# Spreading the background work of a deformable convolution over its units, and finding the largest offset in one pass

## The chip, the cores and the metric

The kernel runs on one core of a Trainium2 chip. The metric is the device time of one execution in microseconds (us). Before the change it is 6298.04 us, the median of three runs (6293.81 to 6311.7). The profile that is shown comes from one profiled execution with a span of 6287.0 us.

## The reference

The input x has 4 images of 128 x 128 pixels and 128 channels, in f32. Four layers follow each other. Each normalises its input by groups of 4 channels, computes something, and adds the result to its input:

```
x = x + relu(deform_conv(gn(x), w_off, b_off, w_def))   # layer 0
x = x + scan_conv1d(gn(x), W)                           # layer 1
x = x + z_self + z_m + z_k                              # layer 2
x = x + triangle(gn(x), ...)                            # layer 3
```

Only layer 0 is touched. It computes, for each pixel, 72 offsets (4 groups of channels x 9 taps x two directions) by a 1x1 convolution of the normalised image:

```
offset = einsum('bchw,oc->bohw', gn(x), w_off) + b_off
val    = bilinear samples of gn(x) at (y + ky - 1 + dy, x + kx - 1 + dx)
out    = relu(einsum('bgckhw,ogck->bohw', val, w_def))
```

A bilinear sample whose offset is at most 1 in size needs only neighbouring pixels. The kernel relies on that. It keeps the largest absolute offset that occurred, and where it is over 1 it computes the layer again by a general path (`deform_general`).

## The kernel before

`deform_layer` works through 172 **blocks**: 4 images of 43 blocks, each of `RY` = 3 rows of the output. A block has `NU` = 4 **units** (L720). In each unit TensorE samples a quarter of the block's columns for all nine taps (`sample_unit`, L525), and ScalarE and VectorE copy the samples out of PSUM into `ring` (L551, L549). Then come the weights of two or three taps of the next block (`next_taps`, which calls `tents`): TensorE makes two factors in `t_ps` (L500, L508), ScalarE copies one of them to SBUF (`tent`, L514), and VectorE multiplies them into `m` (L516). `t_ps` has two buffers, and the next block's `sample_unit` needs all nine taps of `m`. Last comes a quarter of the convolution of the block before (L608). At the end of a block, VectorE adds that convolution's result to the image (`finish`, L578, which writes `x1c`) and so frees its one PSUM buffer, `conv_ps`.

Beside the blocks runs work for later blocks and later layers. Python generators hand it out in small pieces, and the calls in the unit loop (L724 to L732) set how many pieces a unit gets:

- **Preparing rows** (`prepared`, called through `step`). It makes the table of normalised pixels and the offsets of 8 rows, in two groups of 4 rows. A group has seven pieces: four transposes (L403), the normalisation to `rows` (L405), the offset matmul (L416), the scaling on VectorE and GpSimd (L419, L422), and three pieces that split the f32 offsets into three bf16 parts (ScalarE L432, VectorE L434 and L440, GpSimd L438). The first split piece also takes the maximum of the group's offsets, the second the minimum (L434). The two groups and one empty call make 15 steps for 8 rows. `ready[b]` is the number of rows of image `b` that are prepared.
- **Counting the next image** (`count_of`, advanced by `next(beside["count"], None)`). It loads an image in 16 halves of 16 rows into one buffer, `xhalf`, and takes 16 statistics instructions (`bn_stats`, L344) of each half. A half has six pieces: four that only leave time for the transfer, and two of 8 `bn_stats`. Preparing an image can begin once it is counted and `scales_of` has run, which goes through `step` as well.
- **Counting the layer's own output** (`count`, L592). Each 16 rows of output put 32 `bn_stats` into a list, and `count(n)` takes up to n of them. At the first block of the next image the list is emptied.

The order of the instructions on each engine is the order in which the program emits them (`manual_schedule`, L700). After the last block, L761 to L774 reduce `ranges` to a flag that says whether an offset was over 1.

Of the kernel before, what the change touches and what calls it, by code (L numbers as in the profile page):

```python
# [10 lines left out]
F32 = mybir.dt.float32  # L11
# [3 lines left out]
ALU = mybir.AluOpType  # L15
AX = mybir.AxisListType
# [3 lines left out]
P = 128  # L20
B = 4
S = 128
NG = 4
NK = 9
NL = NK * NG
# [3 lines left out]
PADW = S + 2  # L29
# [10 lines left out]
RY, RX = 3, 4  # L40
# [148 lines left out]
def deform_layer(tc, c, small, x, w_off, b_off, w_def, x1, tabs, offs):  # L189
# [11 lines left out]
    nc = tc.nc  # L201
    RC = 16
    RP = 8
    RO = 4
    NROWS = 1 + NG * NPART
    NB = RY * PADW
    with ExitStack() as ctx:
        wp = ctx.enter_context(tc.tile_pool(name="l0w", bufs=1))
# [14 lines left out]
        nc.tensor.matmul(wsum_ps, lhsT=woff, rhs=c.ones[:, 0:1], start=True, stop=True)  # L223
        wsum = wp.tile([2 * NL, 1], F32, name="wsum")
        nc.vector.tensor_copy(wsum, wsum_ps)
        ranges = wp.tile([2 * NL, 2, B * S // RO], F32, name="ranges")

# [4 lines left out]
        with tc.tile_pool(name="l0prep", bufs=1) as prep:  # L234
# [14 lines left out]
            for d in range(2):  # L249
                for place in range(RX):  # L250
                    for after, factors in ((-1, (-1, 1, 0)), (0, (1, -2, 1)), (1, (0, 1, 0))):
                        at = place + 1 + after
# [14 lines left out]
            for q in range(4):  # L267
                p0 = 32 * q
                nc.scalar.dma_start(spread[p0 : p0 + 1, q % 2], picks[0:1, q // 2, 2])
                for n in range(NPART):  # L270
                    p1 = p0 + 1 + n
                    nc.scalar.dma_start(
                        spread[p1 : p0 + NROWS : NPART, q % 2], picks[:, q // 2, n // NSPLIT]
                    )
# [44 lines left out]
        for t in pixels:  # L319
            nc.vector.memset(t, 0.0)  # L320

        ring = wp.tile([P, 3 * RY, NK, PADW], F32, name="ring")

        def ring_rows(n, r0, r1):
            at = (n * RY + r0) % (3 * RY)
            return ring[:, at : at + r1 - r0]

        parts = wp.tile([2 * NL, NPART, RP, OW], BF16, name="parts")
# [53 lines left out]
        def load_group(n):  # L382

            if n not in loaded and n < B * S // RO:
                b, y = n * RO // S, n * RO % S
                loaded[n] = three.tile([P, RO, S], F32, name="xin")
                nc.sync.dma_start(loaded[n], x[b, :, y : y + RO, :])

        def prepared(b, y0):

            s, t, st, koff = scales[b]
            table = tabs[b].rearrange("x (r s) c -> x r s c", s=SX)
            for h in range(0, RP, RO):
                n = (b * S + y0 + h) // RO
                load_group(n)
                load_group(n + 1)
                load_group(n + 2)
                xc = loaded.pop(n)
                if h == 0:
                    rows = one.tile([P, 2 * RO, P], F32, name="rows")  # L400
                pt = ps_g.tile([P, RO, P], F32, name="img_ps", tag="gn_ps")
                for i in range(RO):
                    nc.tensor.transpose(pt[:, i], xc[:, i, :], c.ident)  # L403
                yield
                nc.scalar.activation(rows[:, h : h + RO], pt, AF.Identity, bias=t, scale=s)  # L405
                if h + RO == RP:
                    for q in range(RX):
                        src = rows[q:S:RX]
                        for x0, at in ((0, q + 2), (1, q - 2)):
                            if at >= 0:  # L410
                                nc.sync.dma_start(
                                    table[x0 : x0 + NXB - 1, 2 + y0 : 2 + y0 + RP, at, :], src
                                )
                yield
                po = ps_g.tile([2 * NL, RO, S], F32, name="off_ps", tag="gn_ps")
                nc.tensor.matmul(po, lhsT=woff, rhs=xc, start=True, stop=True)  # L416
                yield
                off = one.tile([2 * NL, RO, S], F32, name="off")
                nc.vector.tensor_tensor(  # L419
                    off, po, st[:, 0].unsqueeze(1).to_broadcast([2 * NL, RO, S]), ALU.mult  # L420
                )
                nc.gpsimd.tensor_tensor(  # L422
                    off, off, koff.unsqueeze(1).to_broadcast([2 * NL, RO, S]), ALU.add
                )
                yield
                flat = off.rearrange("p r c -> p (r c)")

                rest = one.tile([2 * NL, RO, S], F32, name="rest")
                left = off
                for i in range(NSPLIT):  # L430
                    part = parts[:, i, h : h + RO, 2 : S + 2]
                    nc.scalar.copy(part, left)  # L432
                    if i < 2:
                        nc.vector.tensor_reduce(  # L434
                            ranges[:, i, n : n + 1], flat, AX.X, (ALU.max, ALU.min)[i]
                        )
                    if i + 1 < NSPLIT:
                        nc.gpsimd.tensor_tensor(rest, left, part, ALU.subtract)  # L438
                        left = rest
                    nc.vector.scalar_tensor_tensor(  # L440
                        parts[:, NSPLIT + i, h : h + RO, 2 : S + 2], off, 0.0, part,
                        ALU.is_gt, ALU.mult,
                    )
                    yield
            at = (y0 + 2) * OW
            nc.sync.dma_start(
                offs[b].rearrange("(l n) c -> l n c", n=NPART)[:, :, at : at + RP * OW],
                parts.rearrange("l n r c -> l n (r c)"),
            )
            ready[b] = y0 + RP  # L450

        def load_parts(t, b, j, rows, taps):

            for d in range(2):
                for kx in range(3):
# [3 lines left out]
                    nc.sync.dma_start(  # L459
                        t[p0 : p0 + NROWS - 1, k0 : k0 + len(taps)].rearrange(  # L460
                            "p k r c -> p k (r c)"
# [128 lines left out]
        def count(n):  # L590
            for _ in range(min(n, len(to_count))):
                nc.vector.bn_stats(*to_count.pop(0))  # L592
# [23 lines left out]
        def terms_of(n, j):  # L616

            if j == 0:
                return 0, 1, [(ky, 0, ring_rows(n, ky, ky + 1)) for ky in (2, 1, 0)]
            terms = []  # L620
            for ky in (2, 1, 0):
                at = 0
                for r0, r1 in ((ky - 2, 0), (0, ky + 1)) if n % 3 == 0 else ((ky - 2, ky + 1),):
                    if r0 < r1:
                        terms.append((ky, at, ring_rows(n, r0, r1)))
                        at += r1 - r0
            return RY * j - 2, RY * j + 1, terms
# [5 lines left out]
        ready = [0] * B  # L633
        beside = {"now": None, "norms": [], "rows": 0, "count": iter(())}
# [77 lines left out]
        for n, (b, j) in enumerate(blocks):  # L712
            load_row(n + 2)
            if n + 1 < len(blocks):
                pixel_tiles[n + 1] = load_pixels(*blocks[n + 1])
            pix = pixel_tiles.pop(n)
            m = ms.pop(("m", n)).rearrange("p r k c -> p (r k) c")
            end = j + 1 == NYB
            v = ring_rows(n, 0, RY).rearrange("p r k c -> p (r k) c")
            for i in range(NU):  # L720
                sample_unit(m, pix, v, i)
                next_taps(2)
                next(convs, None)
                for _ in range(4 if ready[b] < min(S, RY * j + 26) else 2):  # L724
                    step()
                next_taps((i == 0) + (end and i > 0))
                count(12)
                if not (j == 0 and i == 0):
                    for _ in range(2):
                        next(beside["count"], None)  # L730
                elif b + 1 < B:
                    beside["count"] = counting(b + 1)  # L732
            for _ in convs:
                pass
            if j == 0:
                if b:
                    count(len(to_count))
                    beside["norms"].append(x1_norm(b - 1, stats))
                stats = one.tile([P, NGN, S // RC, 6], F32, name="stats1")
            if not end:  # L740
                convs = convolved(b, *terms_of(n, j), stats, NU)
            else:
                ve = one.tile([P, 1, 3, PADW], F32, name="ve")
                sample_row(ms.pop(("me", n))[:, 0], pix, ve[:, 0])
                convs = chain(
                    convolved(b, *terms_of(n, j), stats, NU // 2),
                    convolved(
                        b, S - 1, S,
                        [(2, 0, ve), (1, 0, ring_rows(n, 2, 3)), (0, 0, ring_rows(n, 1, 2))],
                        stats, NU // 2,  # L750
                    ),
                )
# [5 lines left out]
            pass  # L758


        ends = wp.tile([2 * NL, 2], F32, name="ends")  # L761
        nc.vector.tensor_reduce(ends[:, 0:1], ranges[:, 0], AX.X, ALU.max)
        nc.vector.tensor_reduce(ends[:, 1:2], ranges[:, 1], AX.X, ALU.min)
        most = wp.tile([2 * NL, 1], F32, name="most")
        nc.vector.scalar_tensor_tensor(most, ends[:, 1:2], -1.0, ends[:, 0:1], ALU.mult, ALU.max)
        most_ps = ps_g.tile([1, 2 * NL], F32, name="most_ps", tag="gn_ps")
        nc.tensor.matmul(
            most_ps, lhsT=most, rhs=c.ident[0 : 2 * NL, 0 : 2 * NL], start=True, stop=True
# [711 lines left out]
```

## Time and profile before

The page's shares are over the whole span; layer 0 is about half of it. The table has the stretches that matter. A block ends where VectorE makes its one copy of line 553, so the times of those 172 copies in the trace give the length of every block.

| what | value |
|---|---|
| PE, DVE, ACT, POOL busy, whole span | 85%, 55%, 39%, 16% |
| ends of the first and the last block | 211.9 us, 3273.3 us |
| TensorE clock granted, whole span | 0.934 |
| one tensor_reduce of line 434, 72 x 512 f32 | 672 ns, 256 of them |
| one bn_stats of line 344 or 592 | 209 ns, 768 and 1024 of them |
| transposes, off matmuls of a group of 4 rows | line 403 and line 416, 128 groups |

[...] twelve bn_stats in a row take 1.60 us in the timeline, which is 0.13 us each.

### The profile page before, as it was taken

Reading aid. Unit: us, or ns where it says so; the run is one execution under the profiler, and the core shown is the slowest. Engines: PE = TensorE matmul, PEld = TensorE weight load, DVE = VectorE, ACT = ScalarE, POOL = GpSimd, SP = SyncE. Lnnn points to the kernel's source line nnn. Section 1 sums busy time; section 2 is a strip of 40 time slices with the busy share of each in tenths; the row PEclk is TensorE's granted clock in tenths of the full one; section 3 lists DMA queues with packets and bytes.
Section 4 is the critical chain, followed back from the end, with each engine's and each line's share of the span. In section 5 each row is a group of like instructions: output and inputs, shape, how many; then the busy total and the mean of one; then the engine's idle time right before and its main releaser. Section 6 shows DMA issues by size and latency. Waiting matters only on the chain. (4 is left out here: it accounts for less than half of the span.)

```text
span 6287.0 us, 157182 instructions
## 1 busy us (share of the span) xinstructions
PE 5363.7 (85%) x67400; PEld 4503.6 (72%) x67400; DVE 3485.6 (55%) x7296; ACT 2422.6 (39%) x4709; POOL 990.9 (16%) x714
## 2 busy tenths in 40 slices
PE   0689899889889898999998999998787887877876
PEld 0577778777778777788887888887474674664765
DVE  6576666666666666655544444445547446446442
ACT  0344454445444454444431111111433534434433
POOL 0211221112220122100000000000205114114122
PEclk9899998999999999999999999999998988989987
DMA  3575655665556565544432112211515416316314
GB/s 115 125 158 127 138 133 126 146 131 129 134 132 129 114 138 130 121 92 83 90 77 85 62 60 67 68 65 47 172 44 194 139 49 207 121 56 209 111 60 134
DMA packets 1264569, 710.30 MB, mean 113 GB/s; under 512 B 844621, under 2 KB 1111150, under 8 KB 1254646
## 3 DMA queue, kind: packets, MB, share of 16 engines
q1 hardware_dynamic: 1234322, 658.55, 41.3%
q10 hardware_dynamic: 29540, 41.60, 1.9%
q8 instruction: 532, 8.72, 0.6%
q14 instruction: 175, 1.43, 0.1%
HBM read 417.28 MB, written 282.55 MB: 111 GB/s over the span
## 5 line engine op out<-in xcount | busy, mean ns | idle before, releaser
L608 PE MATMUL conv_ps<-ring,wdef 128*128 128x192 f32 (+2 forms) x7632 | 1342.3, 326 | 75.7 <-DVE x1c L578 75.7
L608 PEld LDWEIGHTS conv_ps<-ring,wdef 128*128 128x128 f32 x7632 | 1168.2, 199 | 189.5 <-issue 103.5
L516 DVE TENSOR_TENSOR m<-t_ps,tent 128x390 f32<-128x390 f32 x1548 | 814.3, 559 | 803.9 <-ACT tent L514 774.6
L1075 PE MATMUL conv_ps<-carry,wconv 128*128 128x256 f32 x4572 | 1011.3, 378 | 0.3 <-issue 0.3
L1075 PEld LDWEIGHTS conv_ps<-carry,wconv 128*128 128x128 f32 x4572 | 852.1, 189 | 121.9 <-issue 0.6
L500 PE MATMUL t_ps<-parts_of,spread 57*64 57x99 bf16 (+1 forms) x12384 | 801.3, 277 | 105.5 <-DVE m L516 80.9
L525 PE MATMUL v_ps<-m,pixels 60*64 60x108 f32 (+1 forms) x22704 | 770.8, 267 | 114.8 <-DVE m L516 104.0
L514 ACT COPY tent<-t_ps 128x390 f32<-128x390 f32 x1560 | 709.7, 492 | 358.7 <-PE t_ps L500 356.3
L551 ACT COPY ring<-v_ps 128x432 f32<-128x432 f32 x1032 | 503.8, 523 | 855.1 <-PE v_ps L525 849.0
L525 PEld LDWEIGHTS v_ps<-m,pixels 60*64 60x64 f32 x22704 | 635.4, 138 | 271.0 <-DVE m L516 134.1
L500 PEld LDWEIGHTS <-spread 57*64 57x64 bf16 x12480 | 643.2, 127 | 192.1 <-issue 168.4
L1057 ACT ACTIVATE rowT<-x1T_ps,t_x,s_x 128x128 f32<-128x128 f32 x512 | 192.2, 457 | 864.6 <-PE x1T_ps L1053 417.0
L1320 PEld LDWEIGHTS pair_ps<-wcat,X 128*128 128x128 f32 x4096 | 474.2, 192 | 37.2 <-DVE T L1326 14.6
L1320 PE MATMUL pair_ps<-wcat,X 128*128 128x128 f32 x4096 | 494.8, 279 | 5.5 <-POOL X L1307 3.6
L508 PE MATMUL t_ps<-parts_of,spread 57*64 57x130 bf16 x9288 | 497.1, 227 | 0.0
L1326 DVE TENSOR_TENSOR T<-pair_ps,sig 128x512 f32<-128x512 f32 x256 | 266.6, 1044 | 398.0 <-ACT sig L1325 397.8
L422 POOL TENSOR_TENSOR off<-off,koff 72x512 f32<-72x512 f32 x128 | 163.0, 1273 | 1948.1 <-DVE off L419 1948.1
L1228 POOL TENSOR_TENSOR zc<-z 128x1024 f32<-128x1024 f32 x64 | 130.0, 2032 | 1824.2 <-DVE z L1221 1728.8
L1086 DVE SCALAR_TENSOR_TENSOR carry<-conv_ps,rowT 128x256 f32<-128x256 f32 x254 | 107.3, 423 | 540.4 <-PE conv_ps L1075 540.4
L508 PEld LDWEIGHTS <-spread 57*64 57x64 bf16 x9312 | 393.0, 109 | 0.0
L1390 PE MATMUL one_ps<-outw,y 128*128 128x128 f32 x1024 | 249.8, 333 | 150.5 <-POOL y L1384 150.0
L440 DVE SCALAR_TENSOR_TENSOR parts<-off,parts 72x512 bf16<-72x512 f32 x384 | 341.4, 891 | 28.4 <-ACT parts L432 21.2
(179 smaller groups left out, 6204.7 us busy)
## 6 DMA issues: line engine op xcount, KB each, us to landing
pixels<-tab SPq DMA_DIRECT2D x688, 123.8 KB
parts_of<-off SPq DMA_DIRECT2D x1032, 55.7 KB
off<-parts SPq DMA_DIRECT2D x64, 891.0 KB
tab<-rows SPq DMA_DIRECT2D x384, 128.0 KB
xin<-in_x_dram SPq DMA_DIRECT2D x128, 256.0 KB
x<-x1c SPq DMA_DIRECT2D x32, 1024.0 KB
x1rows<-x SPq DMA_DIRECT2D x128, 256.0 KB
x2T<-x2c ACTq DMA_DIRECT2D x128, 256.0 KB
```

Source lines behind the costliest of these rows:

```text
L440: nc.vector.scalar_tensor_tensor(parts[:, NSPLIT + i, h : h + RO, 2 : S + 2], off, 0.0, part, ALU.is_gt, ALU.mult,)
L500: nc.tensor.matmul(tp[h : h + HALF, 0, 0:n].rearrange("p (r c) -> p r c", c=PADW)[:, :, i:PADW:RX], lhsT=spread[0:k, kx // 2, i, h : h + H ...
L508: nc.tensor.matmul(tp[h : h + HALF, 1, i * PADW : (i + 1) * PADW], lhsT=spread[HALF : HALF + k, kx // 2, first + i, h : h + HALF], rhs=src ...
L514: nc.scalar.copy(tent[:, 0:n], tp[:, 0, 0:n])
L516: nc.vector.tensor_tensor(m, *pair, ALU.mult)
L525: nc.tensor.matmul(to[p1 : p1 + HALF], lhsT=pix[p0 : p0 + LANES, xb, :], rhs=m[p0 : p0 + LANES, :, RX * xb : RX * xb + w], start=True, sto ...
L551: nc.scalar.copy(to, bodies[side])
L608: nc.tensor.matmul(pc[:, at : at + rows, x0:x1], lhsT=wdef[:, side, k, :], rhs=v[:, :, k if v.shape[2] == NK else kx, x0 + kx : x1 + kx], ...
L1075: nc.tensor.matmul(pc, lhsT=wt[:, k, :], rhs=old[h][:, :, k : k + S], start=(k == 0), stop=(k == TAPS - 1),)
L1320: nc.tensor.matmul(pj[:, j], lhsT=X[:, j0 + j, :], rhs=wcat[:, q * 4 * DQ : (q + 1) * 4 * DQ], start=True, stop=True,)
L1326: nc.vector.tensor_tensor(T[:, q : NQ + 1 : NQ - q, :, j0 : j0 + JB], pj[:, :, 0 : 2 * DQ].rearrange("p j (n d) -> p n d j", n=2), sig.rea ...
L1390: nc.tensor.matmul(po[:, j], lhsT=y[:, j], rhs=outw, start=False, stop=True)
```

## The change

The change does four things in layer 0, all in `deform_layer`.

- The work for the output's statistics is taken two instructions per unit and not up to twelve.
- The count of the next image gets one piece per unit and not two.
- When fewer rows are ready than the lead asks for, a unit takes three steps of preparing and not four. The lead is 18 rows ahead of the block and not 26. Otherwise a unit takes two steps, as before.
- The largest offset is found by one maximum over absolute values. The minimum of each group goes, and with it one reduce and one combination after the last block. `ranges` shrinks to half.

The number of row sets in the ring gets a name, `NRING` = 3, with the same value.

```
-        ranges = wp.tile([2 * NL, 2, B * S // RO], F32, name="ranges")
+        ranges = wp.tile([2 * NL, B * S // RO], F32, name="ranges")
...
-                    if i < 2:
+                    if i == 0:
                         nc.vector.tensor_reduce(
-                            ranges[:, i, n : n + 1], flat, AX.X, (ALU.max, ALU.min)[i]
+                            ranges[:, n : n + 1], flat, AX.X, ALU.max, apply_absolute_value=True
                         )
...
                 next_taps(2)
                 next(convs, None)
-                for _ in range(4 if ready[b] < min(S, RY * j + 26) else 2):
+                for _ in range(3 if ready[b] < min(S, RY * j + 18) else 2):
                     step()
                 next_taps((i == 0) + (end and i > 0))
-                count(12)
+                count(2)
                 if not (j == 0 and i == 0):
-                    for _ in range(2):
-                        next(beside["count"], None)
+                    next(beside["count"], None)
                 elif b + 1 < B:
                     beside["count"] = counting(b + 1)
...
-        ends = wp.tile([2 * NL, 2], F32, name="ends")
-        nc.vector.tensor_reduce(ends[:, 0:1], ranges[:, 0], AX.X, ALU.max)
-        nc.vector.tensor_reduce(ends[:, 1:2], ranges[:, 1], AX.X, ALU.min)
         most = wp.tile([2 * NL, 1], F32, name="most")
-        nc.vector.scalar_tensor_tensor(most, ends[:, 1:2], -1.0, ends[:, 0:1], ALU.mult, ALU.max)
+        nc.vector.tensor_reduce(most, ranges, AX.X, ALU.max)
```

More of the change, by code (lines that the diff above doesn't have):

```diff
@@ L204, in deform_layer @@
     RO = 4
+    NRING = 3
     NROWS = 1 + NG * NPART
@@ L320, in deform_layer @@
             nc.vector.memset(t, 0.0)
-        ring = wp.tile([P, 3 * RY, NK, PADW], F32, name="ring")
+        ring = wp.tile([P, NRING * RY, NK, PADW], F32, name="ring")
         def ring_rows(n, r0, r1):
-            at = (n * RY + r0) % (3 * RY)
+            at = (n * RY + r0) % (NRING * RY)
             return ring[:, at : at + r1 - r0]
@@ L622, in terms_of @@
                 at = 0
-                for r0, r1 in ((ky - 2, 0), (0, ky + 1)) if n % 3 == 0 else ((ky - 2, ky + 1),):
+                for r0, r1 in ((ky - 2, 0), (0, ky + 1)) if n % NRING == 0 else ((ky - 2, ky + 1),):
                     if r0 < r1:
```

## The prediction, made before the changed kernel had run

> **What bounds the kernel now.** I read the page's slices first: layer 0 runs from about 212 to 3273 us. The ends of the 172 copies of line 553 on VectorE then give each block's length. By what runs beside the blocks they fall into four kinds, and the windows view of such stretches separates them (its columns are busy times of PE, PEld, DVE, ACT and POOL, the clock, the DMA share, GB/s):
>
> ```profile
> core 0: us, PE busy (x) PEld busy (x) DVE busy (x) ACT busy (x) POOL busy (x), PEclk, DMA share, GB/s
> 286.20:465.80 179.60, 152.15 (x2772) 130.33 (x2772) 128.65 (x416) 81.39 (x173) 34.44 (x29) 0.93 0.66 149
> 1090.00:1295.90 205.90, 174.56 (x3111) 150.33 (x3110) 140.10 (x438) 91.59 (x196) 40.94 (x33) 0.93 0.66 143
> 488.70:1000.10 511.40, 460.57 (x8639) 394.78 (x8639) 327.03 (x706) 253.07 (x538) 108.92 (x88) 0.96 0.57 131
> 1349.00:1827.50 478.50, 427.40 (x8009) 366.52 (x8010) 307.32 (x670) 236.28 (x503) 104.06 (x84) 0.96 0.59 133
> 2102.00:2612.90 510.90, 456.02 (x8652) 390.20 (x8651) 326.59 (x707) 252.81 (x538) 108.96 (x88) 0.97 0.57 132
> 1920.70:2079.90 159.20, 149.19 (x3018) 133.04 (x3018) 100.71 (x404) 66.98 (x151) 0.00 (x0) 0.97 0.59 113
> 2703.10:3261.80 558.70, 557.42 (x11779) 499.09 (x11780) 282.28 (x736) 259.63 (x587) 0.00 (x0) 1.00 0.45 87
> ```
>
> - Nothing beside but the output's statistics (last row, 39 blocks): 558.7 / 39 = 14.32 us a block, PE busy all of it, clock 1.00. This is TensorE's own floor.
> - Preparing rows (three rows before the last two; 28, 26 and 28 blocks): 1500.8 / 82 = 18.30 us.
> - Preparing and counting the next image (first two rows; 9 and 10 blocks): 19.96 and 20.59 us.
> - Counting alone (row before the last, 10 blocks): 15.92 us.
>
> TensorE sets the time where nothing runs beside it. Elsewhere it stands still: over 212 to 3273 us a window shows it busy 2775.75 of 3061 us, so 285 us are idle. The waits of PE in 488.7 to 1000.1 us say for whom:
>
> ```profile
> PE v_ps L525 <- DVE m L516: 18.9, 12, 4.4
> PE t_ps L500 <- DVE m L516: 18.1, 14, 2.2
> PE conv_ps L608 <- DVE x1c L578: 12.5, 8, 2.0
> ```
>
> (us in total, times, longest.) All three are VectorE results. VectorE is only about 64% busy there, so its mean load is not the limit; the limit is **bursts** that stand ahead of `m` and `x1c` in its queue. The timeline of VectorE shows one, with the instruction that the change removes elsewhere in the same queue:
>
> ```profile
> 772.37 1.02 DVE L516 TENSOR_TENSOR m<-t_ps,tent 128x390 f32<-128x390 f32 x2
> 773.31 1.60 DVE L592 BATCH_NORM_STATS2 stats<-x1c 128x6 f32<-128x64 f32 x12
> 775.69 1.03 DVE L516 TENSOR_TENSOR m<-t_ps,tent 128x390 f32<-128x390 f32 x2 [0.77 <-ACT tent L514]
> 776.64 0.68 DVE L419 TENSOR_TENSOR off<-off_ps,st 72x512 f32<-72x512 f32 x1
> 778.71 0.68 DVE L434 TENSOR_REDUCE ranges<-off 72x1 f32<-72x512 f32 x1 [1.39 <-POOL off L422]
> ```
>
> [...] PE waits up to 4.4 us for `m` while VectorE is busy with side work.
> [...]
>
> **The change part by part.** How many pieces each unit gets, I counted by stepping through the loop's generators; for the kernel before this gives the trace's counts in each block, to within a block.
>
> 1. *The minimum.* 128 reduces of line 434 go, about 122 of them beside blocks. Start to start one holds VectorE 0.60 us (761.31 to 761.91 in the timeline), so 122 x 0.60 = 73 us of VectorE. How much of it reaches TensorE? The preparing blocks without a burst in them or in the block before (50 of them) take 18.03 us. A group's own TensorE work is 0.63 us of transposes and 1.03 us of off matmul (lines 403 and 416, 31 groups in 466 to 1018 us: 19.4 and 32.0 us); at 1.07 groups a block, 1.77. So 18.03 - 14.32 - 1.77 = 1.9 us a block is loss, for some 4.4 x 1.07 = 4.7 us of VectorE work (0.61 for line 419, two reduces of 0.60, three of line 440 at about 0.85). That is 0.4 us lost per us of side work; 0.60 x 0.4 x 122 = 30 us. Ends: 0 (the reduce only fills VectorE's wait for ScalarE's next part) and 73. The maximum stays at 0.67 us; were the absolute value a second pass, the reduce would double and the gain be 0.
>
> 2. *Output statistics, 2 a unit.* Bursts of 12, 12 and 8 (1.6, 1.6, 1.1 us) become 0.26 us in each of 16 units; a unit is 3.6 us. In preparing blocks the bursts cost 18.30 - 18.03 = 0.27 us a block, over 82 blocks 22 us. Beside no preparing they cost nothing (last window). I take two thirds, 14; ends 0 and 22. The list still empties: 32 per 5.3 blocks come, 8 a block can go, four blocks before the next come. The flush at an image's end stays.
>
> 3. *Counting, one piece a unit.* Half a buffer's 16 statistics came in one unit (2.1 us); now 8 each in two neighbouring units. Counting lasts 24 blocks, not 12. So blocks with both preparing and counting rise from 28 to 51, counting alone from 11 to 21; the statistics that meet preparing are as many, 544 of 768. The cost now: (19.96 - 18.03) x 9 + (20.59 - 18.03) x 10 + (15.92 - 14.32) x 10 = 17 + 26 + 16 = 59 us, collisions with output bursts included. The new cost is unknown. Most in one unit falls from 12 + 16 to 2 + 8, some 1.3 us, which is within the two-buffer slack of `t_ps`, but beside an unlucky pair of steps not free. Bounds: nothing, or the same per statistic (59). I take 0.5 us in 51 blocks and 0.1 in 21: 27 us, a gain of 32.
>
> 4. *Preparing.* Steps stay at two per unit nearly everywhere, since the lead is reached in the first blocks of image 0. Before, five groups fall in its blocks 1 to 3 (74.3 us), now three. The first of two groups in a block costs more than a single one: (74.3 - 3 x 14.32) / 5 = 6.3 us with the counting, against 3.7 = 1.9 + 1.8; two moved groups save 5 us. Because counting ends later, preparing pauses in images 1 and 2 (their blocks 15 to 25) and runs on to block 13 of image 3, whose blocks are now at the floor. That moves time between images and costs nothing in sum: 128 groups stay 128. The shortest distance is 13 rows at a block's start, against the 9 that `load_row` asks for, so no new wait.
>
> 5. *End.* One 0.27 us reduce and a combination go, about 0.6 us. `NRING` is a name. Transfers are the same; the one on `xhalf` gets four units where it had two, so VectorE's 9.3 us of waiting for it goes (in part 3).
>
> Sum: 30 + 14 + 32 + 5 + 1 = 82 us; 6298 - 82 = **6216 us**. Nothing after 3273 us changes.
>
> **The rivals.**
> - *Everything is recovered.* The slack swallows all side work: 73 + 22 + 59 + 5 + 1 = 160, so 6138 us. For it: 285 us of idle PE and a clock below 1.00 that would rise. Against: blocks with no burst still lose 1.9 us, and most of that (scaling, splitting) stays.
> - *Spreading only moves the loss.* Twice as many blocks carry preparing and counting together, each losing half as much; the output's statistics now meet every preparing step. Then only the minimum and the small terms count: 30 + 5 + 1 = 36, so 6262 us; 6292 if the minimum only filled a wait.
> - *Slower.* VectorE never catches up: where bursts were followed by blocks of recovery (17.74 us after a burst, against 18.03), now every one of 119 preparing blocks (68 + 51) carries 8 to 24 statistics. If each lost 0.4 us more, 48 us, and the minimum gained nothing: 6298 + 48 - 6 = 6340. Against: VectorE's mean load per unit, about 3.3 us, stays under TensorE's 4.0.
>
> **How the numbers follow.** Forecast 0.55, all recovered 0.2, only moved 0.16, slower 0.09. The time is the forecast's. The range is from 6135, where everything is recovered, to 6285, where spreading gives nothing and the minimum little. 0.3% is 19 us, so same is 6279 to 6317: the bottom of the third case, 0.05, and a little of the slow one, 0.02. Faster 0.86, same 0.07, slower 0.07.
>
> **What would show it.** Line 434 should be 128 instructions still near 0.67 us; 1.3 would sink part 1. Preparing blocks with no counting should take about 17.8 us, those with counting about 18.3, the floor 14.32. PE's waits for `m` and `x1c` should fall from 285 us of idle in the stretch to some 200. POOL should show a gap in image 1 and one in image 2, and work at the start of image 3. What would make the prediction wrong: blocks with counting that still take 20 us, or preparing blocks whose loss does not follow VectorE's work but a wait that the change leaves alone.

## The result, and the profile after

The changed kernel takes 6225.84 us (median of four runs, 6223.58 to 6229.97) against 6304.87 us for the kernel before (four runs, the three of the first section among them). The ratio is 0.9876, with a 95% interval of 0.9857 to 0.9896, which is 78 us (66 to 90) less. The forecast was 82 us less, and 6216 us lies 10 us below the measured median.

Layer 0 carries all of it: its blocks ended at 3273.3 us and now end at 3203.5 us, 70 us earlier, and the spans of the two profiled executions differ by 65 us. (A trace is one execution. That of the kernel before took 6289.14 us, 16 us under the median, so sums over its blocks can differ by some 15 us from gains by medians.) The windows view of the changed kernel, with the columns as in the prediction, shows the same four kinds of stretch. The first two rows have preparing and counting (image 0, blocks 4 to 24; image 1, blocks 3 to 15), the next two preparing alone (image 0, blocks 27 to 41; image 3, blocks 4 to 14), the fifth counting alone (image 1, blocks 16 to 23), and the last neither:

```profile
271.40:649.50 378.10, 343.35 (x6474) 294.55 (x6472) 249.34 (x721) 191.12 (x404) 90.37 (x67) 0.96 0.69 153
1052.10:1293.50 241.40, 216.36 (x4015) 186.64 (x4015) 153.82 (x439) 118.14 (x251) 57.94 (x42) 0.95 0.66 142
687.60:958.90 271.30, 247.21 (x4638) 212.09 (x4638) 159.78 (x368) 135.79 (x289) 66.12 (x47) 0.96 0.58 131
2603.30:2805.30 202.00, 185.59 (x3397) 160.22 (x3398) 115.64 (x250) 99.83 (x214) 49.56 (x36) 0.93 0.54 125
1293.50:1407.50 114.00, 113.70 (x2407) 101.50 (x2407) 67.61 (x234) 53.26 (x121) 0.00 (x0) 1.00 0.65 126
2805.30:3192.00 386.70, 385.73 (x8155) 345.29 (x8156) 195.62 (x522) 179.80 (x407) 0.00 (x0) 1.00 0.47 90
```

The fifth row is the clearest. Counting alone now leaves TensorE busy 113.70 of 114.00 us at a clock of 1.00; a block takes 14.25 us, the floor. Before it took 15.92 us at 0.97. The fourth row shows the work that moved to image 3: GpSimd is busy 49.56 us there, where it had stopped before.

The mean length of a block by kind, from the ends of the copies that close each block, for blocks 3 to 39 of each image and without the few that combine statistics (the number of blocks in brackets). A block is put under counting from the first to the last `bn_stats` of the next image's count, also where that count only waits for its transfer:

| kernel | preparing | preparing and counting | counting | neither | blocks 40 to 42 of images 0 to 2 |
|---|---|---|---|---|---|
| before | 18.27 (77) | 20.69 (19) | 15.82 (8) | 14.38 (38) | 18.58 |
| changed | 17.88 (53) | 18.22 (47) | 14.29 (17) | 14.31 (25) | 21.29 |

TensorE's waits from 212 to 3200 us (total, times, longest), in the kernel before and then in the changed kernel:

```profile
PE v_ps L525 <- DVE m L516: 104.0, 56, 6.3
PE conv_ps L608 <- DVE x1c L578: 82.7, 46, 3.8
PE t_ps L500 <- DVE m L516: 78.8, 65, 6.8
...
PE conv_ps L609 <- DVE x1c L579: 84.4, 48, 6.2
PE v_ps L526 <- DVE m L517: 83.4, 55, 3.2
PE t_ps L501 <- DVE m L517: 57.3, 53, 2.3
```

The waits for `m` fell; those for `x1c` did not.

### The profile page after: what moved, and what is told of

Read it like the earlier page. It is cut to its first block, busy times and chain, and to the rows that moved or that the text cites. A ratio compares the mean times of both kernels' runs of the same rounds, so it can differ in the third digit from the quotient of the medians.

```text
span 6221.7 us, 157053 instructions
## 1 busy us (share of the span) xinstructions
PE 5345.9 (86%) x67400; PEld 4490.3 (72%) x67400; DVE 3362.8 (54%) x7166; ACT 2423.9 (39%) x4709; POOL 1043.8 (17%) x714
## 5 line engine op out<-in xcount | busy, mean ns | idle before, releaser
L526 PE MATMUL v_ps<-m,pixels 60*64 60x108 f32 (+1 forms) x22704 | 757.4, 264 | 89.7 <-DVE m L517 83.4
L501 PEld LDWEIGHTS <-spread 57*64 57x64 bf16 x12480 | 634.1, 125 | 168.7 <-issue 145.6
L509 PEld LDWEIGHTS <-spread 57*64 57x64 bf16 x9312 | 387.9, 108 | 0.0
L441 DVE SCALAR_TENSOR_TENSOR parts<-off,parts 72x512 bf16<-72x512 f32 x384 | 292.4, 762 | 108.7 <-ACT parts L433 95.7
```

The lines of the kernel that those rows point to most:

```text
L441: nc.vector.scalar_tensor_tensor(parts[:, NSPLIT + i, h : h + RO, 2 : S + 2], off, 0.0, part, ALU.is_gt, ALU.mult,)
L501: nc.tensor.matmul(tp[h : h + HALF, 0, 0:n].rearrange("p (r c) -> p r c", c=PADW)[:, :, i:PADW:RX], lhsT=spread[0:k, kx // 2, i, h : h + H ...
L509: nc.tensor.matmul(tp[h : h + HALF, 1, i * PADW : (i + 1) * PADW], lhsT=spread[HALF : HALF + k, kx // 2, first + i, h : h + HALF], rhs=src ...
L526: nc.tensor.matmul(to[p1 : p1 + HALF], lhsT=pix[p0 : p0 + LANES, xb, :], rhs=m[p0 : p0 + LANES, :, RX * xb : RX * xb + w], start=True, sto ...
```

## The experiments

All were timed in five rounds beside the kernel before. A gain in us is one minus the ratio, times 6305; the difference between two versions is that of their ratios, times 6305. Theory A is the forecast, or what would follow from it; the rivals are named in the expectations. Lengths of blocks and waits come from one trace of each version.

### The parts alone

**The minimum alone.** Edit to the kernel before: one maximum over absolute values, as in the change, and nothing else.

```
-                    if i < 2:
+                    if i == 0:
                         nc.vector.tensor_reduce(
-                            ranges[:, i, n : n + 1], flat, AX.X, (ALU.max, ALU.min)[i]
+                            ranges[:, n : n + 1], flat, AX.X, ALU.max, apply_absolute_value=True
```

> Before, with the minimum alone taken away (one maximum over absolute values), all pacing as before. Theory A, the forecast: VectorE's work costs TensorE 0.4 us per us, so 128 reduces of 0.60 us give about 30 us less. Theory B: the minimum stood in VectorE's queue just where it would otherwise wait for ScalarE's second part (the trace after shows 82.7 us of waiting for these parts where before had 28.4), so the time comes back as waiting and the gain is under 15 us. Under B the waits of line 440 for ScalarE's parts rise from 28 us to some 60 to 80 us in this run as well; under A they stay near 28.

Measured: 6279.21 us, ratio 0.9949 (0.9932 to 0.9965), so 32 us (22 to 43). The size is theory A's, but the sign that was to show theory B is there as well. The groups of VectorE's products and of GpSimd's second subtraction, from 212 to 3274 us, first in the kernel before:

```profile
L440 DVE SCALAR_TENSOR_TENSOR parts<-off,parts 72x512 bf16<-72x512 f32 x368 | 329.3, 897 | 17.6 <-ACT parts L432 10.6
L438 POOL TENSOR_TENSOR rest<-rest,parts 72x512 f32<-72x512 f32 x123 | 136.6, 1110 | 101.9 <-ACT parts L432 101.9
```

and without the minimum:

```profile
L440 DVE SCALAR_TENSOR_TENSOR parts<-off,parts 72x512 bf16<-72x512 f32 x368 | 272.6, 743 | 108.0 <-ACT parts L432 95.2
L438 POOL TENSOR_TENSOR rest<-rest,parts 72x512 f32<-72x512 f32 x123 | 191.7, 1558 | 104.3 <-ACT parts L432 104.3
```

(Busy us, mean ns of one, then idle time before and its cause.) VectorE's wait for ScalarE's parts rises from 10.6 to 95.2 us: the minimum had stood where VectorE now waits. Its products get shorter (897 to 743 ns), and GpSimd's subtraction longer (1110 to 1558 ns), and in the lines that the last section shows the product now starts 0.05 us ahead of the subtraction, where it had started 0.39 us behind. So both theories hold in part: 32 us remained of 83 us of reduces.

**The output's statistics alone.** Edit: `count(12)` becomes `count(2)`.

> Before, with the output's statistics alone spread: two a unit instead of up to twelve. Theory A: bursts in preparing blocks cost 22 us, of which two thirds come back, plus a part of the collisions with the counting: 14 to 25 us less. Theory C, spreading only moves the loss: within 8 us of before. In the blocks with counting alone in image 2 the collision bursts (20 and 17 us blocks) vanish under both, since there VectorE has room.

Measured: 6301.3 us, ratio 0.9996 (0.9985 to 1.0006): 2.5 us, not told apart from nothing. Preparing blocks stay at 18.22 us, preparing-and-counting blocks at 20.77, and counting blocks at 15.95. The last falsifies the one point on which both theories agreed, that these bursts cause the counting blocks' loss. In image 2 the longest of them, block 7, holds 6 of the output's statistics here and 32 before, and takes 19.6 us and 20.0. What stays in it is a wait at the head of VectorE's queue for the transfer into `xhalf`. The waits for this transfer in the kernel before and in this run:

```profile
DVE stats L344 <- DMA xhalf<-in_x_dram: 9.3, 5, 3.6
DVE stats L344 <- DMA xhalf<-in_x_dram: 7.6, 5, 4.0
```

The longest of each, 3.6 and 4.0 us, is the one in this block. All six kernels with two pieces of counting a unit have such waits in layer 0 (7.6 to 16.5 us in sum); none of the eight with one piece has any.

**The counting of the next image alone.** Edit: one `next(beside["count"], None)` a unit.

> Before, with the counting of the next image alone slowed to one piece a unit. Theory A: about 25 to 32 us less; blocks with preparing and counting fall from about 20.3 to about 19, since the output's bursts of twelve still meet them. Theory C: twice as many such blocks lose half each, so within 8 us of before.

Measured: 6301.32 us, ratio 0.999 (0.9982 to 0.9999): 6 us (1 to 11). Where the counting runs the gain is there: preparing-and-counting blocks fall to 19.19 us and counting blocks to 14.43. But there are 45 and 18 of them where there were 19 and 8, and blocks 40 to 42 of images 0 to 2 rise from 18.58 to 21.41 us.

**The lead alone.** Edit: `range(3 if ready[b] < min(S, RY * j + 18) else 2)`.

> Before, with three steps and a lead of 18 rows alone. Theories A and C: 5 us less, all of it in the first blocks of image 0 (74 us for blocks 1 to 3 becomes under 65), nothing elsewhere. If the lead had a cost (waits for rows that are not yet written), it would show as waits of TensorE for transfers in those blocks, and the time would be over before.

Measured: 6289.67 us, ratio 0.997 (0.9956 to 0.9985): 19 us (9 to 28), four times the forecast's term. In the trace, blocks 1 to 3 of image 0 take 62.7 us where they took 74.3, and block 0 ends 3.2 us earlier. That is 15 us, in the place that was named.

**Both kinds of counting together.** Edit: the two edits above.

> Before, with both kinds of counting spread: two output statistics a unit and one piece of the next image's counting a unit; the minimum and the lead as before. Alone each gave almost nothing (3 to 6 us). Theory A2: the two kinds of burst collide, and either one alone is enough to overrun VectorE, so that only both together gain: 20 to 35 us less than before, with preparing-and-counting blocks at about 18.5 us and counting-only blocks at the floor of 14.3. Theory C: the sum of the two, under 10 us; the whole change then owes its 79 us to the minimum and the lead.

Measured: 6290.89 us, ratio 0.9983 (0.9971 to 0.9994): 11 us (4 to 18). That is close to the sum of the two, 9 us, so theory A2's collision is not what hid the gain. The blocks show where it went. Counting blocks are at the floor (14.32 us) and preparing-and-counting blocks at 18.89. Their loss before was 19 x (20.69 - 18.27) + 8 x (15.82 - 14.38) = 57 us; now it is 45 x (18.89 - 18.30) = 27 us. About as much is lost in blocks 40 to 42: nine blocks at 21.97 instead of 18.58 us, 31 us.

### What the waits in VectorE's queue cost

**The maximum one piece later.** Edit to the changed kernel:

```
-                    if i == 0:
+                    if i == 1:
                         nc.vector.tensor_reduce(
```

> The changed kernel, with the remaining reduce moved from the first to the second of the three splitting pieces, where the minimum used to be. It then no longer waits for GpSimd's offsets (86 us of VectorE waiting in the changed kernel), and it fills part of the wait for ScalarE's second part (82.7 us). Theory A: a wait at the head of VectorE's queue costs TensorE what work costs, 0.4 us per us, so 86 us gone are some 25 to 35 us less than the changed kernel (about 6195). Theory D: VectorE has a third of its time free, so waiting costs nothing and only work counts; within 10 us of the changed kernel (6216 to 6236).

Measured: 6253.4 us, ratio 0.9926 (0.9914 to 0.9938), 32 us more than the changed kernel, give or take 14. Both theories are wrong here. VectorE's waits in the changed kernel and then in this one:

```profile
DVE ranges L435 <- POOL off L423: 86.0, 62, 1.4
DVE parts L441 <- ACT parts L433: 81.0, 51, 3.7
...
DVE parts L441 <- ACT parts L433: 159.4, 89, 4.0
```

The reduce waits no longer, but the first product, now at its place, waits instead for the same chain. The sum is 159 us after 167. Why the time rose, though the waits did not, was not tried; in the trace VectorE's products take 889 ns on average, where the changed kernel has 765.

**The products one piece later as well.** Edit to the kernel of the last run:

```
                     if i + 1 < NSPLIT:
                         nc.gpsimd.tensor_tensor(rest, left, part, ALU.subtract)
                         left = rest
-                    nc.vector.scalar_tensor_tensor(
-                        parts[:, NSPLIT + i, h : h + RO, 2 : S + 2], off, 0.0, part,
...
+                    if i:
+                        above(i - 1)
                     yield
+                above(NSPLIT - 1)
```

Here `above(i)` is the product of part i that stood in the place of the first call.

> As the run before, and VectorE's product of each split part (line 440 before, 441 after) is emitted one piece later, so that ScalarE has long made the part. Theory A: both waits of VectorE, 86 and 83 us, go, and the time falls by 50 to 65 us below the changed kernel, to about 6165. Theory D: within 10 us of the changed kernel. In between if ScalarE's own waits for GpSimd, which stay, are what delays the tent copies.

Measured: 6133.23 us, ratio 0.973 (0.9717 to 0.9743): 170 us less than before, 92 us less than the changed kernel, which is more than theory A had. Its groups:

```profile
L433 DVE SCALAR_TENSOR_TENSOR parts<-off,parts 72x512 bf16<-72x512 f32 x369 | 283.3, 794 | 6.6 <-ACT parts L440 6.6
L446 POOL TENSOR_TENSOR rest<-off,parts 72x512 f32<-72x512 f32 x123 | 134.5, 1093 | 117.7 <-ACT parts L440 117.7
L446 POOL TENSOR_TENSOR rest<-rest,parts 72x512 f32<-72x512 f32 x123 | 133.8, 1088 | 112.7 <-ACT parts L440 112.7
```

The product's wait is 6.6 us, and GpSimd's subtractions take 1.09 us each, where the changed kernel has 1354 and 1515 ns. Preparing blocks fall from 17.88 to 17.02 us.

**The steps of a unit apart.** Edit to the changed kernel:

```
                 sample_unit(m, pix, v, i)
+                step()
                 next_taps(2)
                 next(convs, None)
-                for _ in range(3 if ready[b] < min(S, RY * j + 18) else 2):
+                for _ in range(2 if ready[b] < min(S, RY * j + 18) else 1):
                     step()
```

> The changed kernel, with the two preparing pieces of a unit taken apart: one after the sampling, the other where both were. The same pieces per unit. GpSimd (1.27 to 1.59 us a piece) then has half a unit, some 1.8 us, to finish before ScalarE and VectorE need its result. Theory A: the waits of ScalarE (166 and 189 us) and VectorE (86 and 83 us) for the chain through GpSimd mostly vanish, and preparing blocks fall from 17.9 to about 17: 60 to 90 us less than the changed kernel. Theory D: waits cost nothing, within 10 us.

Measured: 6139.34 us, ratio 0.9743 (0.9731 to 0.9756): 162 us less than before, 84 us below the changed kernel. The size is theory A's, the road is not. ScalarE's waits for GpSimd fall, from 166 to 47 us for the offsets and from 188 to 152 us for what is left after a subtraction (`rest`). But VectorE's do not vanish: the reduce waits 38 us and the products 156.5 us (in 180 places), together 195 us after 167. GpSimd's subtractions still take 1362 and 1435 ns, against 1093 and 1088 with the late products, so the collision is still there. Preparing blocks take 17.22 us.

### Undoing parts, and putting the moves together

**The lead undone.** The changed kernel with four steps and 26 rows.

> The changed kernel with the lead and the steps of before (four steps, 26 rows); minimum and counting as changed. The lead alone gave 19 us (9 to 28), where the forecast had 5. If that is its own worth, this kernel takes about 6245, 19 us over the changed one; if the forecast's 5 us was right and the rest was the spread between builds, about 6231. If the three parts help each other, more than 6250.

Measured: 6252.72 us, ratio 0.9915 (0.9898 to 0.9931): 54 us less than before, so the lead is worth 25 us in the changed kernel, give or take 16 from the two intervals. Blocks 1 to 3 of image 0 take 78.0 us here and 62.2 in the changed kernel; block 0 ends at 212.4 against 209.2 us. That is 19 us.

**The counting undone.** The changed kernel with `count(12)` and two pieces of counting a unit.

> The changed kernel with the counting of before (twelve output statistics, two pieces of the next image's counting a unit); minimum and lead as changed. Both kinds of counting together were worth 12 us (4 to 18) in the kernel before. If that is all, about 6238. Theory E: without the minimum VectorE has room for the spread statistics that it did not have before, so the spreading is worth more here: 25 to 40 us, about 6250 to 6265, which would be the part of the 79 us that the parts alone do not add up to.

Measured: 6247.85 us, ratio 0.9905 (0.9889 to 0.9922): 60 us less than before, so both kinds of spreading are worth 18 us (give or take 16). That lies between the two answers, and theory E is neither shown nor excluded. Blocks 40 to 42 are back at 18.37 us.

**Both moves together.** The edits of the late products and of the steps apart.

> The changed kernel with both moves that each gained some 90 us: steps taken apart, and the remaining reduce and the products of the parts emitted one piece later. If both remove the same waits of VectorE behind ScalarE and GpSimd, 10 to 40 us below the better of the two (about 6095 to 6125); if they worked on different waits (the late products on VectorE's, the steps apart on ScalarE's), nearly twice the gain, about 6050.

Measured: 6110.12 us, ratio 0.9687 (0.967 to 0.9705): 197 us less than before, 27 us below the late products alone. Apart the two moves gain 92 and 84 us over the changed kernel, together 119, so a good part of what they remove is the same loss. Preparing blocks take 16.93 us. This is the fastest version that was run.

**The late products in the kernel before.** The edit of the products alone, with minimum, counting and lead as before.

> The kernel before with one edit: the products of the split parts are emitted one piece later; minimum, maximum, counting and lead as before. VectorE waits only about 11 us for these parts in the kernel before, since the two reduces stand in front of them. If waits at the head of the queue are what counts, this gains little here, under 25 us, although the late products with the late maximum gained 93 us in the changed kernel; the minimum was then hiding the wait. If the late products gain 80 us or more here too, their worth is not in VectorE's wait for the parts but in when its other instructions get to run.

Measured: 6192.43 us, ratio 0.9814 (0.9799 to 0.9829): 117 us (108 to 126), where under 25 was expected if the recorded wait of 11 us were the measure. The groups:

```profile
L432 DVE SCALAR_TENSOR_TENSOR parts<-off,parts 72x512 bf16<-72x512 f32 x369 | 266.2, 747 | 0.1
L445 POOL TENSOR_TENSOR rest<-rest,parts 72x512 f32<-72x512 f32 x123 | 134.5, 1093 | 115.7 <-ACT parts L439 115.7
L445 POOL TENSOR_TENSOR rest<-off,parts 72x512 f32<-72x512 f32 x122 | 132.7, 1088 | 125.6 <-ACT parts L439 125.6
```

VectorE's products lose 63 us of their 329, GpSimd's subtractions fall from 1345 and 1110 ns to 1088 and 1093, and preparing blocks fall from 18.27 to 17.40 us. So the recorded wait was not the measure. Two things changed at once: product and subtraction no longer start on the same signal, and the last product of a unit moves behind the next unit's `m`. No run took them apart.

## Why the prediction was right, and which of its terms were not

| part | forecast, us | alone, us | when undone, us |
|---|---|---|---|
| minimum | 30 | 32 (22 to 43) | not run |
| output statistics | 14 | 2.5 (-4 to 9) | - |
| counting | 32 | 6 (1 to 11) | - |
| both kinds of counting | 46 | 11 (4 to 18) | 18 |
| lead | 5 | 19 (9 to 28) | 25 |
| all | 82 | 78 (66 to 90) | |

**What bounds the kernel** held in part. PE waits for `m` and `x1c`: over 212 to 3200 us these are 266 us before and 225 after. Its idle time in layer 0 fell from 285 us to 237 (2994.3 - 2757.7); the forecast had some 200. Another 18 us are PE's busy time, which fell from 2776.05 to 2757.74 us for the same 52,870 or so matmuls; the forecast did not price this apart. Preparing blocks came to 17.88 us, where it had 17.8. But that the time follows the amount of VectorE's side work did not hold: the late products take no instruction away, and the kernel before gains 117 us by them.

The prediction also misread one of its lines. It put PE's longest wait, 4.4 us for `m`, down to VectorE's side work. VectorE was busy in 3.3 us of it, but the chain starts on ScalarE, which could not copy the factors because a cast ahead of them waited for the transfer `off<-parts`, which stores the parts of the 8 rows before:

```profile
780.48 0.62 ACT L432 CAST parts<-off 72x512 bf16<-72x512 f32 x1 [4.43 <-DMA off<-parts]
```

**The minimum** came in at its size. The reduce that is left shows that the absolute value costs no second pass (median 681 ns, after 672 without it). In the forecast this was an assumption: the kernel before has no such instruction to measure. The line's view in the changed kernel (shortest, median and longest in ns):

```profile
L435 DVE TENSOR_REDUCE ranges<-off x128: 669/681/684, 134.7 to 2795.0; 72x1 f32<-72x512 f32 x128
```

The factor of 0.4 us lost per us of VectorE's work gave the right size here. It hid two things that the run without the minimum shows: the removed work came back as waiting (VectorE's wait for parts is 95.2 us, after 10.6), and the collision with GpSimd moved from VectorE's products (897 to 743 ns) to the second subtraction (1110 to 1558 ns).

**The two countings** are the term that failed. The costs in the counting blocks were right: 0.5 us over a preparing block was assumed, and 18.22 - 17.88 = 0.34 measured in the changed kernel; counting alone was put 0.1 us above the floor and lies on it. What the forecast left out is that a slower count shifts which preparing pieces meet in a unit for the rest of the image. Blocks 40 to 42 went from 18.58 to 21.29 us in the changed kernel, nine blocks, 24 us. The output's statistics, which now stand in these blocks too, are not the reason: the run that spreads them alone takes 19.09 us there, and the run that slows the next image's count alone, with none of them there, takes 21.41. With the slower count, 33 products of parts fall in the nine blocks in that run and not 27, so two more groups; at the forecast's 3.7 us a group I estimate 7 us, which other blocks are spared. Another part is one wait of ScalarE in each image for the transfer of the parts, 4.4 to 6.0 us where it was longest before (blocks 29, 34 and 29) and 1.6 to 4.3 us in the changed kernel (blocks 41, 40 and 40). It moved there and is not new. What the rest is made of was not tried.

The output's bursts were also over-priced: alone they hardly moved a preparing block. Of the 22 us that the forecast read as their cost, 16 stand in those three blocks 29, 34 and 29 (23.0, 23.1 and 23.7 us, against 18.03). They do hold a burst, but they also hold ScalarE's wait for the transfer. The run that spreads the bursts keeps that wait, and the three still take 21.5 to 22.7 us. The waits for this transfer from 204 to 3300 us, in the kernel before, in that run and in the changed kernel:

```profile
ACT parts L432 <- DMA off<-parts: 20.1, 4, 6.0
ACT parts L432 <- DMA off<-parts: 19.2, 4, 5.6
ACT parts L433 <- DMA off<-parts: 8.6, 3, 4.3
```

**The lead** was under-sized. The step "two moved groups save 5 us" took 3.7 us as the cost of a group elsewhere and 6.3 in the first blocks; the traces show 15 and 19 us saved in blocks 0 to 3. Blocks 1 to 3 hold the scalings of five groups before and of four after, not three; the other moved group left block 0. And the forecast had no term for a wait: in block 1 of image 0, ScalarE's cast waits for the transfer that still reads `parts`. This is one of the four waits of the kernel before above. It takes 5.2 to 5.8 us in all seven kernels with four steps, and none of the seven with three steps has it. What else makes up the 15 to 19 us was not taken apart.

So the two wrong terms, 28 to 35 us too much and 14 to 20 too little, nearly cancel; that the total lies within 4 us of the forecast is in part luck. The parts alone add up to 62 us of the 78; the intervals are too wide to say whether the other 16 are real. The rival in which spreading only moves the loss was nearer on the counting itself (11 to 18 of 46 us) and wrong on the whole, because the counting gave that much and the lead more than its 5 us.

## What to carry to other kernels

Price spread side work by what each unit then holds, over the whole run and not only where it is counted: a changed pace shifts the phase of everything else that is handed out (here blocks 40 to 42 rose from 18.58 to 21.41 us when the count alone was slowed). Before work is taken off a queue, ask what the next instruction waits for: without the minimum, VectorE's wait for ScalarE's parts rose from 10.6 to 95.2 us. Where a burst and a wait for a transfer fall in the same blocks, look which of the two stays when the burst is gone. And try to emit an instruction that needs a chain over two other engines one piece later, even where its recorded wait is short: here that was worth 92 us in the changed kernel, where a reduce moved as well, and 117 us in the kernel before, where the recorded wait was 10.6 us. The last is more than the whole change. Which part of it is the order in VectorE's queue and which the collision with GpSimd stays open.

## What the runs showed of the hardware

VectorE's products of parts and GpSimd's subtractions slow each other, and which of them is slowed depends on which starts first. In each pair of lines VectorE's product and GpSimd's subtraction read what the same cast of ScalarE wrote. The first two pairs are from the kernel before, the last from the run without the minimum:

```profile
708.31 0.69 DVE L440 SCALAR_TENSOR_TENSOR parts<-off,parts 72x512 bf16<-72x512 f32 x1
708.36 1.59 POOL L438 TENSOR_TENSOR rest<-off,parts 72x512 f32<-72x512 f32 x1 [0.73 <-ACT parts L432]
...
710.68 1.08 POOL L438 TENSOR_TENSOR rest<-rest,parts 72x512 f32<-72x512 f32 x1 [0.73 <-ACT parts L432]
711.07 2.06 DVE L440 SCALAR_TENSOR_TENSOR parts<-off,parts 72x512 bf16<-72x512 f32 x2
...
708.48 0.69 DVE L440 SCALAR_TENSOR_TENSOR parts<-off,parts 72x512 bf16<-72x512 f32 x1
708.53 1.59 POOL L438 TENSOR_TENSOR rest<-rest,parts 72x512 f32<-72x512 f32 x1 [0.73 <-ACT parts L432]
```

Where VectorE's product starts 0.05 us ahead, the subtraction takes 1.59 us (0.64 us until the product ends and the 1.08 us of the second pair would make 1.7, so a subtraction that stands still until then is a rough estimate of it); where GpSimd starts first, it takes 1.08, and two products take 2.06 us together, against 0.69 for the one that started first.

All that start from 212 to 3274 us in the traces of the kernel before and of the changed kernel:

| instruction | before, mean ns (number) | changed, mean ns (number) |
|---|---|---|
| subtraction that starts while a product runs | 1593 (68) | 1596 (168) |
| other subtractions | 1086 (177) | 1086 (78) |
| product that starts while a subtraction runs | 1169 (162) | 1062 (77) |
| other products | 683 (206) | 687 (292) |
| reduce that overlaps a subtraction | 672 (176) | 672 (58) |
| other reduces | 681 (69) | 682 (65) |

The reduce is not slowed in these traces. By what the two engines hold each other up was not shown. The forecast had not counted on the removal of a reduce to change who starts first. In the second pair the minimum, 0.67 us from 710.48 us on, held VectorE's product back until GpSimd had started; without it, in the third pair, the product starts first, and GpSimd's second subtraction takes 1558 ns on average where it took 1110.
